# A softplus table by another name, and column sums added along the rows of y

## The chip, the core and the metric

The kernel runs on one core of a Trainium2 chip. The core has engines that run side by side, each with a queue of its own[...]: TensorE (PE: matmuls, results in PSUM), VectorE (DVE: elementwise work and scans), ScalarE (ACT: activation functions), GpSimd (POOL), and SyncE (SP), which here only issues DMA transfers. Engines wait for each other through semaphores. The metric is the device time of the whole program in microseconds; less is better.

## The reference

Four layers run one after the other on a tensor of 4 images, 192 channels, 56 x 56 pixels. The change lies in the fourth, a selective scan over the image in four directions (L is the number of pixels, D the channels, N = 4 states):

```
xs = stack([x_hw, x_wh, x_hw[..., ::-1], x_wh[..., ::-1]])       # by rows, by columns, both reversed
dts, Bv, Cv = split(einsum('kcd,bkdl->bkcl', x_proj_w, xs))
dt = softplus(einsum('kdr,bkrl->bkdl', dt_proj_w, dts) + dt_proj_b)
h  = exp(dt * A) * h + dt * Bv * u          # step by step along L
y_k = sum over the states of h * Cv         # plus Ds * xs
y  = y_0 + flip(y_2) + columns to rows(y_1) + columns to rows(flip(y_3))
out = x + out_proj(layer_norm(y) * silu(z))
```

So each of the four directions gives one value for each channel and pixel, and y is their sum. The values of the two column directions come in the order of columns, while y is kept in the order of rows.

## The kernel before

The 192 channels are kept as two halves of 96 partitions (`h` = 0, 1). An image of 3136 pixels is cut into seven chunks of 448 (`SCH`): for the row directions (`o == 0`) a chunk is 8 rows of 56, for the column directions (`o == 1`) it is 8 columns of 56. `steps` lists image, direction and chunk: for each image the rows forward, the columns forward, the columns backward, the rows backward, seven steps each.

The work of the layer is written as Python generators. `begin` makes the inputs of a row chunk (layer norm, projection, a 3 x 3 convolution as nine matmuls of L1851, Silu); `begin_columns` makes the products of the column directions with the matmuls of L1893 and the copy of L1896; `load` fetches a step's inputs; `sizes` makes dt for two steps at a time, with a matmul (L1985) and a Softplus (L1997); `decay` spreads dt over the states by DMA (L2023) and takes exp (L2031); `scan` does the rest; `final` normalizes y (matmuls of L1768, VectorE at L1770 and L1789, ScalarE at L1912, matmuls of L1929) and writes the output.

In `scan`, for one half of one step: VectorE multiplies dt and u into `du` (L2046 for rows, L2049 for columns, where u is read 56 floats apart); PE spreads `du` over the states (L2056); VectorE multiplies by B in place in PSUM (L2062) and scans (L2078); GpSimd multiplies by C (L2085); PE sums the four states into a PSUM bank `py` (L2101); and VectorE adds that to `y`: at L2106 for the first direction, at L2111 for the rows backward, at L2114 for both column directions.

The order of all instructions comes from `Order`, a planner that runs while the program is built. Each piece of work names an engine and a cost; `Order.run` picks the piece that could start first and writes it into the queues. ScalarE's functions come from table sets, of which one is loaded at a time. A piece may name the set that it needs. If it differs from the last name, the planner counts `SWITCH` = 1.3 us and issues a load of that set (the line of the helper shows as L315 in the profile):

```
            if table and table != self.table:
                self.table = table
                self.nc.scalar.preload_act_table_set(table)
```

Where an activation finds that the set before it doesn't hold its function, a load is put in front of it when the program is compiled, and stands under the activation's own line. The names are constants (L349 and L350); layer 4 uses `EXP_LN`, `SILU` and `SOFTPLUS`.

Of the kernel before, what the change touches and what calls it, by code (L numbers as in the profile page):

```python
# [19 lines left out]
B, C, H, W = 4, 192, 56, 56  # L20
HW = H * W
HALF = 96
# [214 lines left out]
def rows2(ap, w=W):  # L237
    return ap.rearrange("p (y x) -> p y x", x=w)


class Order:
# [20 lines left out]
    def take(self, kind="bank"):  # L262
        slot = min((s for s in self.kinds[kind] if s[0] is not None), key=lambda s: s[0])
        slot[0] = None
        return slot[1]

    def done(self, tile):

        (slot,) = (s for slots in self.kinds.values() for s in slots if s[1] is tile)
        slot[0] = self.end + self.LATENCY  # L270
# [53 lines left out]
def on_pe(n, *takes, ready=None):  # L324

    return "PE", 0.0019 * n, takes, None, ready


def on_dve(*n, takes=(), ready=None):
    return "DVE", sum(0.08 + 0.00105 * i for i in n), takes, None, ready  # L330


def on_scan(n, ready):
    return "DVE", 0.1 + 0.0023 * n, ("st",), None, ready
# [6 lines left out]
def on_pool(*n, each=0.0011):  # L341
    return "POOL", sum(0.2 + each * i for i in n), (), None, None
# [4 lines left out]


EXP_LN, GELU = "natural_log_exp_and_others", "gelu_and_others"  # L349
SILU, SOFTPLUS = "silu_and_others", "softplus_and_others"  # L350


def layers01(tc, x_in, packs, aps, dst):
# [1322 lines left out]
def layer3(tc, src, packs, aps, dst):  # L1676
# [7 lines left out]
    nc = tc.nc  # L1684
    with ExitStack() as ctx:
# [74 lines left out]
        def gone(*what):  # L1760
            return what in passed
# [244 lines left out]
        def use(t, h):  # L2006

            users[t, h] = users.get((t, h), 0) + 1
            if users[t, h] == 2:
                done(sized[t][0][h])  # L2010
# [23 lines left out]
        def scan(t, h):  # L2034

            b, o, s, c = steps[t]
            u = us[b % 2]
            head = c == (NSC - 1 if s else 0)
            last = c == (0 if s else NSC - 1)
            px = slice(c * SCH, (c + 1) * SCH)  # L2040
            yield lambda: t in sized and (2 * t + h == 0 or gone("multiplied", 2 * t + h - 1))
            dts, b_, c_ = sized[t]
            yield on_dve(SCH, takes=("du",))
            du = take("du")
            if o == 0:
                nc.vector.tensor_mul(du, dts[h], u[:HALF, h, px])  # L2046
            else:
                uv = u[:HALF, h].rearrange("p (y x) -> p x y", x=W)[:, 8 * c : 8 * c + 8]
                nc.vector.tensor_mul(rows2(du, H), rows2(dts[h], H), uv)  # L2049
            use(t, h)  # L2050

            yield on_pe(500, *["bank"] * 3)
            tiles = [take() for _ in range(3)]
            for j in range(3):
                r = slice(32 * j, 32 * j + 32)
                nc.tensor.matmul(tiles[j][:, :SCH], w["c96.rep"][r], du[r], start=True, stop=True)  # L2056
            done(du)
            passed.add(("multiplied", 2 * t + h))
            ends = []
            for j in range(3):  # L2060
                yield on_dve(SCH, ready=order.end if j else None)
                nc.vector.tensor_mul(tiles[j][:, :SCH], tiles[j][:, :SCH], b_)  # L2062
                ends.append(order.end + order.LATENCY)
            if h == 1:
                done(b_)
            das, sts = [], []
            for j in range(3):
                g = 3 * h + j
                yield lambda: (t, h, j) in decays and (head or (t - 1, g) in states)
                da, at = decays.pop((t, h, j))  # L2070
                yield on_scan(SCH, ready=max(at, ends[j]))
                sts.append(take("st"))
                r = slice(None, None, -1 if s else 1)
                first = 0.0
                if not head:
                    before = states.pop((t - 1, g))
                    first = before[:, 0:1] if s else before[:, SCH - 1 : SCH]
                nc.vector.tensor_tensor_scan(  # L2078
                    sts[j][:, r], da[:, r], tiles[j][:, :SCH][:, r], first, ALU.mult, ALU.add
                )  # L2080
                done(tiles[j])
                if not head:
                    done(before)
                yield on_pool(SCH, each=0.0021)
                nc.gpsimd.tensor_mul(da, sts[j], c_)  # L2085
                das.append(da)
                if last:
                    done(sts[j])
                else:
                    states[t, g] = sts[j]  # L2090
            if h == 1:
                done(c_)
                del sized[t]

            yield lambda: b == 0 or gone("read", b - 1, c if (o, s) == (0, 0) else 0)
            yield lambda: (o, s) == (0, 0) or len(started) == 2 * NSC * (b + 1)
            yield lambda: s == 0 or o == 1 or added[b] >= 6 * NSC + 2 * (NSC - 1 - c) + h
            yield on_pe(600, "bank")
            py = take()
            for j in range(3):  # L2100
                nc.tensor.matmul(py[32 * j : 32 * j + 32, :SCH], w["c128.sum"], das[j], start=True, stop=True)  # L2101
                done(das[j])
            yield on_dve(SCH)
            sums = py[:HALF, :SCH]
            if (o, s) == (0, 0):
                nc.vector.scalar_tensor_tensor(  # L2106
                    y[:HALF, h, px], u[:HALF, h, px], d_sum[:, h : h + 1], sums, ALU.mult, ALU.add
                )
                started.add((t, h))
            elif o == 0:  # L2110
                nc.vector.tensor_add(y[:HALF, h, px], y[:HALF, h, px], sums)  # L2111
            else:
                yv = y[:HALF, h].rearrange("p (y x) -> p x y", x=W)[:, 8 * c : 8 * c + 8]
                nc.vector.tensor_add(yv, yv, rows2(sums, H))  # L2114
            done(py)
            added[b] += 1
            if o == 0 and s == 1 and h == 1:
                passed.add(("summed", b, c))
            if added[b] == 8 * NSC:
                passed.add(("scanned", b))  # L2120
# [9 lines left out]
        for t in range(len(steps)):  # L2130
            order.add(2 * t - 5, load(t))
            if t % 2 == 0:
                order.add(2 * t - 3, sizes((t, t + 1)))
            for h in range(2):
                order.add(2 * t + h - 1, decay(t, h))
                order.add(2 * t + h, scan(t, h))
# [35 lines left out]
```

## Time and profile before

| | |
|---|---|
| median of 3 runs | 7017.2 us (7013.4 to 7018.1) |
| the profiled execution | 7014.4 us |
| its span, first to last instruction | 7012.6 us |
| last layer, about | 5050 to 7013 us |
| busy in the span: PE / DVE / ACT / POOL | 5931.5 / 5950.0 / 2699.1 / 1408.0 us |
| table loads under L315 | 358 of 1.283 us |
| table loads under L1997 | 71 of 1.283 us |
| add of L2114 (columns) | 112 of 0.982 us |
| add of L2111 (rows) | 56 of 0.607 us |

The profile is of one execution. A row of a group gives line, engine, operation, the tiles written and read, their shape and number; then, behind the bar, the time that the group kept its engine busy and the mean of one in ns; then how long the engine sat idle before such instructions and what ended that. A row of a stretch gives its limits, its length, and the busy time of each engine in it with the number of instructions, then the granted TensorE clock, the busy share of the DMA engines and what they moved. In the chain of waits a row is start, length and what ran; "issue" is time in which the engine waited for nothing that the profile shows. A row of a line's own view gives shortest, median and longest in ns.

### The profile page before, as it was taken

How to read it: one execution, taken by the hardware profiler on the slowest of the kernel's cores; microseconds unless marked ns; L12 is line 12 of the kernel's file. 1: busy time of each engine (PE TensorE's matmuls, PEld its weight loads, DVE VectorE, ACT ScalarE, POOL GpSimd, SP SyncE). 2: the span in 40 equal slices, each digit the busy share in tenths (PEclk: the TensorE clock that was granted, in tenths of full speed). 3: DMA queues.
4: the chain of work that ended last, by engine and by line, in shares of the span. 5: the costliest groups of instructions: out<-in, count | busy, mean ns of one | idle time of the engine just before them, and what ended most of it. 6: DMA issues, size and time to landing. Idle time of an engine off the chain costs nothing.

```text
span 7012.6 us, 107574 instructions
## 1 busy us (share of the span) xinstructions
PE 5931.5 (85%) x43810; PEld 2703.5 (39%) x43810; DVE 5950.0 (85%) x7379; ACT 2699.1 (38%) x4134; POOL 1408.0 (20%) x1409
## 2 busy tenths in 40 slices
PE   4999989999999994877888888875888999888856
PEld 2444444444544441344444454442322322222212
DVE  2799999999999999548999989997269779698697
ACT  1111111222212221144455555553356666566544
POOL 0000000000000000032222122210235445355354
PEclk9999989999999997989999999997999999999977
DMA  3222112221222112210000000000246555465454
GB/s 93 56 52 68 31 32 60 52 68 29 63 51 66 35 43 70 64 32 16 17 20 15 19 16 19 18 13 7 60 116 152 135 130 147 115 151 147 118 131 112
DMA packets 252043, 462.68 MB, mean 66 GB/s; under 512 B 30388, under 2 KB 237964, under 8 KB 240412
## 3 DMA queue, kind: packets, MB, share of 16 engines
q1 hardware_dynamic: 251548, 455.80, 25.6%
q8 instruction: 345, 5.65, 0.3%
q14 instruction: 150, 1.23, 0.1%
HBM read 238.58 MB, written 62.96 MB: 43 GB/s over the span
## 4 chain that ended last, share of the span: by engine, by line
DVE 47%; PE 36%; issue 7%; ACT 5%; POOL 2%; DMA 2%; SPq 0%; DVEq 0%; POOLq 0%; ACTq 0%
DVE pr L789 9%; DVE oa L794 6%; PE a_bank L634 5%; DVE bg L1343 5%; PE c_bank L1851 4%; DVE ob L794 4%; DVE st L2078 3%; DVE bxn L1343 3%; PE c_bank L2056 2%; PE a_bank L884 2%; PE a_bank L869 2%; PE c_bank L1893 2%; PE c_bank L2101 2%; DVE c_bank L2062 2%; PE c_bank L1929 2%
## 5 line engine op out<-in xcount | busy, mean ns | idle before, releaser
L789 DVE TENSOR_TENSOR pr<-vdx,attn 112x1792 f32<-112x1792 f32 (+4 forms) x720 | 1185.9, 1649 | 19.0
L634 PE MATMUL a_bank<-qk_in,w_a 64*49 64x392 f32 x9408 | 1158.6, 496 | 0.0
L2085 POOL TENSOR_TENSOR da<-st,bc 128x448 f32<-128x448 f32 x672 | 845.4, 1267 | 884.9 <-DVE st L2078 793.7
L794 DVE TENSOR_TENSOR oa<-oa,pr 112x1792 f32<-112x1792 f32 (+1 forms) x423 | 765.1, 1809 | 0.0
L634 PE MATMUL a_bank<-qk_in,wd 64*49 64x392 f32 x4032 | 694.6, 496 | 0.0
L2078 DVE TENSOR_TENSOR_SCAN st<-da,st,c_bank 128x448 f32<-128x448 f32 x576 | 644.7, 1133 | 20.9 <-issue 12.7
L634 PEld LDWEIGHTS a_bank<-qk_in,w_a 64*49 64x49 f32 x9408 | 431.7, 120 | 395.9 <-issue 391.2
masks.py:197 POOL MEMSET b_ident<- 128x128 f32 x1 | 0.2, 206 | 2861.2 <-DVE sc L1042 2861.2
L2031 ACT ACTIVATE da<-da,a_neg 128x448 f32<-128x448 f32 x672 | 407.4, 658 | 155.8 <-DMA da<-dt 144.6
L315 ACT ACT_TABLE_LOAD x358 | 459.3, 1283 | 6.2
L2062 DVE TENSOR_TENSOR c_bank<-c_bank,bc 128x448 f32<-128x448 f32 x672 | 385.3, 619 | 75.3 <-PE c_bank L2056 74.5
L2056 PE MATMUL c_bank<-du,w_c 32*128 32x448 f32 x1344 | 291.3, 663 | 173.9 <-DVE du L2049 96.4
L1343 DVE SCALAR_TENSOR_TENSOR bg<-bzpad,w_b,bg 128x448 f32<-128x448 f32 (+2 forms) x672 | 421.8, 682 | 0.0
L1851 PE MATMUL c_bank<-pad,diag 128*96 128x448 f32 (+2 forms) x1008 | 413.0, 549 | 2.4 <-ACT pad L1832 2.4
L2101 PE MATMUL c_bank<-da,w_c 128*32 128x448 f32 x1344 | 343.8, 612 | 73.9 <-POOL da L2085 60.3
L794 DVE TENSOR_TENSOR ob<-ob,pr 112x1792 f32<-112x1792 f32 (+3 forms) x282 | 393.3, 1395 | 0.0
L869 PE MATMUL a_bank<-xc,w_a 128*128 128x448 f32 x672 | 300.8, 577 | 70.2 <-DVE xc L854 70.2
L878 ACT ACTIVATE hm<-a_bank,w_a 128x448 f32<-128x448 f32 x168 | 106.4, 634 | 644.9 <-PE a_bank L869 619.1
L634 PEld LDWEIGHTS a_bank<-qk_in,wd 64*49 64x49 f32 x4032 | 249.1, 120 | 256.4 <-issue 254.5
L1432 PE MATMUL bank<-bxn,w_b 128*128 128x448 f32 (+2 forms) x672 | 295.0, 567 | 16.7 <-DVE bxn L1215 16.3
L884 PE MATMUL a_bank<-hm,w_a 128*96 128x448 f32 x672 | 289.3, 562 | 21.1 <-ACT hm L878 21.1
L586 ACT ACTIVATE qk_in<-a_bank,qk_bias,qk_scale 64x224 f32<-64x224 f32 (+5 forms) x288 | 146.3, 526 | 412.2 <-PE a_bank L571 409.9
(306 smaller groups left out, 10091.6 us busy)
## 6 DMA issues: line engine op xcount, KB each, us to landing
da<-dt SPq DMA_DIRECT2D x672, 224.0 KB
vdx<-vmem SPq DMA_DIRECT2D x168, 476.0 KB
bc<-prod SPq DMA_DIRECT2D x224, 224.0 KB
row<-x SPq DMA_DIRECT2D x56, 336.0 KB
x<-x SPq DMA_DIRECT2D x4, 2352.0 KB
vmem<-vt SPq DMA_DIRECT2D x56, 168.0 KB
xc<-x SPq DMA_DIRECT2D x56, 168.0 KB
mid<-xc SPq DMA_DIRECT2D x56, 168.0 KB
```

The costliest lines, as they stand in the source:

```text
L315: self.nc.scalar.preload_act_table_set(table)
L634: nc.tensor.matmul(py[a][outs[g], : 7 * W].rearrange("p (y x) -> p y x", x=W), wt[halves[a], dx], q[halves[a], r, i0 + m : i0 + m + 7, dx ...
L789: nc.vector.tensor_mul(pr, vv, wt)
L794: nc.vector.tensor_add(og, og, before)
L869: nc.tensor.matmul(ph[:, :CH], w["a128.c1T"][:, k, 128 * m : 128 * m + 128], xt[:, k], start=(k == 0), stop=(k == 1),)
L1343: nc.vector.scalar_tensor_tensor(dst, x, wt[:, t : t + 1], dst, ALU.mult, ALU.add)
L1851: nc.tensor.matmul(rows2(pc[:HALF, : n * W]), diag[:, h, t], pad[:, h, at + t // 3 : at + t // 3 + n, t % 3 : t % 3 + W], start=(t == 0), ...
L2056: nc.tensor.matmul(tiles[j][:, :SCH], w["c96.rep"][r], du[r], start=True, stop=True)
L2062: nc.vector.tensor_mul(tiles[j][:, :SCH], tiles[j][:, :SCH], b_)
L2078: nc.vector.tensor_tensor_scan(sts[j][:, r], da[:, r], tiles[j][:, :SCH][:, r], first, ALU.mult, ALU.add)
L2085: nc.gpsimd.tensor_mul(da, sts[j], c_)
L2101: nc.tensor.matmul(py[32 * j : 32 * j + 32, :SCH], w["c128.sum"], das[j], start=True, stop=True)
```

## The change

Two edits in the last layer. The constant `SOFTPLUS` names the set "softplus" in place of "softplus_and_others". And the add of L2114 runs through the same elements of `y` in another order: before, along the 56 pixels of a column and then over the 8 columns, with the sums read from PSUM in their own order; after, along 8 neighbours in a row and then over the 56 rows, with the sums read from PSUM 56 floats apart. The number of elements and their values are the same, as are the costs and names that the planner compares.

```
-SILU, SOFTPLUS = "silu_and_others", "softplus_and_others"
+SILU, SOFTPLUS = "silu_and_others", "softplus"
...
             else:
-                yv = y[:HALF, h].rearrange("p (y x) -> p x y", x=W)[:, 8 * c : 8 * c + 8]
-                nc.vector.tensor_add(yv, yv, rows2(sums, H))
+
+                yv = y[:HALF, h].rearrange("p (y x) -> p y x", x=W)[:, :, 8 * c : 8 * c + 8]
+                nc.vector.tensor_add(yv, yv, sums.rearrange("p (x y) -> p y x", y=H))
             done(py)
```

## The prediction

> **What bounds the kernel now.** I began with the page: the program is a row of stages, and both edits act in the last layer alone (about 5050 to 7013 us), so whole-span shares say little. I cut that stretch at the places where the column-direction steps begin and end, and asked for the busy time of each engine in each piece.
>
> ```profile
> core 0: us, PE busy (x) PEld busy (x) DVE busy (x) ACT busy (x) POOL busy (x), PEclk, DMA share, GB/s
> 5050.00:5230.00 180.00, 168.45 (x494) 52.82 (x492) 102.67 (x136) 105.85 (x147) 58.11 (x54) 0.97 0.45 113
> 5230.00:5425.00 195.00, 169.81 (x585) 49.79 (x586) 187.60 (x230) 122.70 (x176) 108.54 (x89) 0.95 0.59 147
> ...
> 6190.00:6390.00 200.00, 172.42 (x598) 50.22 (x593) 192.25 (x237) 127.18 (x183) 111.73 (x93) 0.95 0.60 150
> ...
> 6675.00:6880.00 205.00, 126.02 (x400) 29.50 (x400) 188.36 (x228) 93.78 (x135) 115.71 (x86) 0.74 0.53 132
> ```
>
> The first row is a row-direction piece: PE works 168 of 180 us, and DVE has room. The other three are column pieces, and there are four, one for each image: DVE works 187.6 of 195, 188.2 of 196, 192.3 of 200 and 188.4 of 205 us, while PE has 25 us or more free. So the columns are VectorE's and the rows are TensorE's. In the first column piece the longest wait of PE is for VectorE: 16.2 us, before the matmuls of L2056, for `du` of L2049. ScalarE is nowhere full (at most 64%), so table loads cost only where others stand still for them.
>
> Next the groups by line, shapes kept apart, and the single lines of the two edits:
>
> ```profile
> L2062 DVE TENSOR_TENSOR c_bank<-c_bank,bc 128x448 f32<-128x448 f32 x672 | 385.3, 619 | 75.3 <-PE c_bank L2056 74.5
> ...
> L2049 DVE TENSOR_TENSOR du<-dt,u 96x448 f32<-96x448 f32 x112 | 113.6, 1014 | 0.0
> L2114 DVE TENSOR_TENSOR y<-y,c_bank 96x448 f32<-96x448 f32 x112 | 109.9, 982 | 12.9 <-PE c_bank L2101 12.6
> ...
> L2111 DVE TENSOR_TENSOR y<-y,c_bank 96x448 f32<-96x448 f32 x56 | 34.0, 607 | 30.6 <-PE c_bank L2101 30.6
> ```
>
> ```profile
> L1997 ACT ACT_TABLE_LOAD  x71: 1283/1283/1283, 5050.2 to 6915.4; - x71
> ```
>
> ```profile
> L1655 DVE TENSOR_TENSOR bacc<-bacc,bank x400: 401/409/420, 3063.3 to 4737.0; 96x256 f32<-96x256 f32 x134
> ```
>
> L2114 is the edited add. L2111 is the same add for the row directions, same sizes and memories, without a stride: 607 against 982 ns. The second fence is a table load under the line of the Softplus itself, 71 times; the third is an add of the layer before, which edit 2 needs. Last the chain of waits, where one of them stands:
>
> ```profile
> 5169.77 1.28 ACT L315
> 5171.05 0.01 issue
> 5171.06 1.28 ACT L1997
> 5172.34 0.01 issue
> 5172.35 0.64 ACT dt L1997
> 5172.99 0.02 issue
> 5173.02 0.63 DVE du L2046
> ```
>
> Two loads run back to back: the one that the planner asks for (L315), and then another under L1997. The first does nothing useful.
>
> **What the edits leave alone.** The planner sees table names only as equal or unequal and charges one SWITCH for a change; the add's cost is `on_dve(SCH)` both times. So the order of every queue, SP's and POOL's too, stays as it is; no instruction or DMA is moved or added, and no semaphore wait is new. Shorter work in an unchanged order lets later work start earlier, never later, unless it collides: the `da` transfers behind a Softplus (SP, L2023) start up to 1.3 us sooner, with DMA busy 0.45 to 0.6, which has room.
>
> **Edit 1, the table name.** If "softplus" holds the function, the 71 loads under L1997 go: 71 x 1.283 = 91.1 us of ScalarE. The loads back to exp and ln (L315) stay. Identity, as in the activations of L1912 that follow a Softplus, already runs from the softplus table, so no load comes back there. What is it worth? Reading the chain through the last layer, 13 of the 71 lie on it, ten in full and three for 0.15 us with the rest put under "issue", so at most 13 x 1.283 = 16.7 us. In the place shown, `du` and the matmuls of L2056 follow the Softplus within 0.04 us each, so all of the load is won there, and the next late thing is the copy of the products (L1896) ahead of it. Elsewhere it is the matmul that feeds the Softplus: in the last image nine Softplus wait another 2.8 to 5.2 us for L1985 after the load, which is then hidden whole. How close the next cover stands at the 13 the chain does not say. Bounds 0 (nothing is added that could cost) and 16.7; I take 11, two thirds.
>
> The Trainium skill, page "ScalarE: Activation LUTs", section "What ACT_TABLE_LOAD costs", adds a drain of about 1.38 us to each switch, 2.66 in all. Here the Softplus starts 12 ns after the load ends in 53 of 71 cases, so the trace has no such drain. By the page the 13 would be worth 34.6 us, by the trace 16.7; I use the trace.
>
> **Edit 2, the add.** Before, `y` is read and written in SBUF 56 floats apart and the sums stream from PSUM in order. After, `y` goes in runs of 8 floats, and the sums are read from PSUM 56 floats apart. Runs of 8 in SBUF cost nothing: L1655 reads and writes such runs with its other operand in PSUM, and needs 409 ns for 256 elements, against 607 for 448. The two differ by 198 ns for 192 elements, 1.03 ns each, as in a plain stream. The strided PSUM read is the unknown, as no VectorE row of this trace has one.
> Low end: it is free, 607 ns (no less, since 448 elements at 1.03 ns leave no room below), a gain of 112 x 0.375 = 42 us of VectorE. High end: it costs what the SBUF stride does, or more. L2049 strides one read only and takes as long as L2114 (medians 981 and 982), so one strided read is enough to lose the gain.
> Against the change stands the skill: "Advanced Engine Details and Errata", section "PSUM Cachelines", gives PSUM lines of 8 bytes, and wants every two elements in a row for best throughput. Every element would now be on a line of its own: 982 ns stays, or more. For the change stands L2062: it reads and writes PSUM in place, two accesses for each element, at 619 ns, no slower than L2111 with one. So PSUM has some access rate to spare, where the SBUF rows show none that covers a stride. I take 607 ns as the likelier, at six in ten, no more.
>
> Of the 42 us, how much shows? Low: the chain has pieces of L2114 in 50 places, 50 x 0.375 = 18.8 us. High: in the column pieces VectorE is busy 756 of 796 us, 95%, and 0.95 x 42 = 40. Between 5280 and 5330 us five of eight adds are on the chain, which would make 26. Once VectorE is 10 us shorter an image, PE (170 of 195) and the POOL products (L2085) set more of the steps. I take 24.
>
> **Sum.** 24 + 11 = 35 us. The profiled execution took 7014.4 us (span 7012.6 and 1.8 around it), 2.8 below the median of 7017.2; a 35 us cut makes it 6979 and the median 6982. A measurement of this kernel tells about 0.2%, 14 us, from no change.
>
> **The rivals.**
> - *PSUM stride costs as in SBUF* (982 stays): only the loads count, 0 to 17, middle 11: 7006, which is mostly no change. For it the skill's rule; against it L2062.
> - *PSUM stride costs two steps*: lines half as wide, so 607 + 2 x 375 = 1357 ns, 375 more than now. It falls in the column pieces, where VectorE is the bound; 70% of 112 adds on the way to the end (the cover shrinks as VectorE grows) make 78 x 0.375 = +29, less 11 for the loads: +18, 7035. It turns slower from about 11 / 78 = 0.14 us above 982, so from 1.12 us an add. For it: the skill's narrower lines. Against it: the one known stride costs just one step.
> - *The name doesn't do what it says*: "softplus" too is followed by a load under L1997. Then only the add counts, about 24: 6993. The profile cannot exclude it; it shows only that the present name doesn't serve.
>
> **How the numbers follow.** Full-rate PSUM read 0.60, its own range 6968 (all 16.7 and some 32 of the add) to 7001 (18.8 with no load); PSUM as SBUF 0.26; two steps 0.10; useless name 0.04. Faster by over 0.2%: 0.58 + 0.07 of the second case + 0.03 = 0.68. Within 0.2%: 0.02 + 0.18 + 0.01 + 0.01 = 0.22, one term for each case in this order. Slower: 0.09 of the two-step case and 0.01 of the second. The range 6968 to 7015 takes in the first two cases and leaves out the two-step one, with a few tails.
>
> **What would show it right or wrong.** L1997 should have no ACT_TABLE_LOAD left, and L315 still 358. L2114's successor (L2115, as a line is added) should stand near 607 ns; 980 or 1350 decides for a rival. VectorE's busy time should fall by 42 us and the four column pieces shorten by 5 to 8 us each, with more waits of L2062 for the matmuls of L2056. ScalarE should lose 91 us of busy time for about 11 of the span. The prediction fails if the add is at 607 and the column pieces keep their length, or if PE's waits grow by as much as VectorE saves.

## The result, and the profile after

The changed kernel took 6971.6 us (median of 5 runs, 6968.4 to 6974.9) against 7017.2 before: a ratio of 0.9936, with an interval of 0.9921 to 0.9950. That is 45.6 us less. In a second set of runs the same pair gave 0.9949 (0.9935 to 0.9962), 37.5 us. The forecast was 35 us, in a range that holds both.

The page of the profile after, its first lines, and the rows of the two edits (the views of the lines themselves, then the groups of the last layer with their shapes):

```profile
span 6966.6 us, 107498 instructions
## 1 busy us (share of the span) xinstructions
PE 5909.1 (85%) x43810; PEld 2697.8 (39%) x43810; DVE 5902.2 (85%) x7379; ACT 2605.9 (37%) x4063; POOL 1402.8 (20%) x1409
```

```profile
L2115 DVE TENSOR_TENSOR y<-y,c_bank x112: 581/600/619, 5215.9 to 6825.4; 96x448 f32<-96x448 f32 x112
```

```profile
L315 ACT ACT_TABLE_LOAD  x358: 1283/1283/1283, 207.7 to 6871.5; - x179
```

```profile
L2062 DVE TENSOR_TENSOR c_bank<-c_bank,bc 128x448 f32<-128x448 f32 x672 | 384.6, 617 | 89.7 <-PE c_bank L2056 89.3
...
L1997 ACT ACTIVATE dt<-c_bank,w_c 96x448 f32<-96x448 f32 x224 | 128.9, 625 | 132.3 <-PE c_bank L1985 130.6 <-DVE du L2046 0.8
...
L2115 DVE TENSOR_TENSOR y<-y,c_bank 96x448 f32<-96x448 f32 x112 | 67.3, 601 | 16.4 <-PE c_bank L2101 16.3
```

And the row of the Softplus before, with the same shapes, for comparison:

```profile
L1997 ACT ACTIVATE dt<-c_bank,w_c 96x448 f32<-96x448 f32 x224 | 128.9, 626 | 73.6 <-PE c_bank L1985 72.4
```

Both edits do what they say. The add is at 600 ns (before 982) and VectorE lost 47.8 us of busy time, 42.6 of it here. All 71 loads under L1997 are gone, ScalarE is 93 us less busy, and L315 still has its 358. But look at what stands in front of the Softplus now: it waits 130.6 us for its matmuls of L1985, where before it waited 72.4. Of the 91 us of loads, 58 became waiting (80 in the pair of experiments below that differs by the name alone and has the new add: 54.8 to 134.8 us). And L2062 waits 89.3 us for L2056, before 74.5, as forecast.

The stretches of the last layer, cut at the first `du` and the last add of an image's columns (the row stage before them, then the columns of the first, third and last image):

```profile
5046.00:5200.30 154.30, 146.88 (x423) 45.74 (x421) 84.95 (x114) 79.64 (x115) 47.50 (x46) 0.98 0.43 109
5200.30:5400.20 199.90, 176.92 (x629) 53.85 (x628) 189.63 (x244) 123.34 (x184) 116.28 (x96) 0.96 0.60 151
6141.30:6342.30 201.00, 177.96 (x629) 54.06 (x628) 189.76 (x245) 123.44 (x184) 116.32 (x96) 0.95 0.60 150
6614.10:6825.40 211.30, 133.91 (x416) 31.44 (x416) 186.69 (x237) 89.83 (x137) 120.78 (x90) 0.69 0.52 130
```

The columns are still VectorE's (190 of 200 us), but the last image gained little: cut in the same way it took 214.5 us before and 211.3 now, at a granted TensorE clock of 0.69. That is the odd one, and the experiments come back to it.

Of the 46.0 us between the two profiled spans, only 34.0 arise in the last layer. It begins (first instruction of L1722) at 4911.0 us in the profile before and at 4899.0 us in the one after, behind layers that the change does not touch.

### The profile page after: what moved, and what is told of

Its sections match the earlier page's. It is cut to its first block, busy times and chain, and to the rows that moved or that the text cites. A ratio compares the mean times of both kernels' runs of the same rounds, so it can differ in the third digit from the quotient of the medians.

```text
span 6966.6 us, 107498 instructions
## 1 busy us (share of the span) xinstructions
PE 5909.1 (85%) x43810; PEld 2697.8 (39%) x43810; DVE 5902.2 (85%) x7379; ACT 2605.9 (37%) x4063; POOL 1402.8 (20%) x1409
## 4 chain that ended last, share of the span: by engine, by line
DVE 46%; PE 38%; issue 6%; ACT 6%; DMA 2%; POOL 2%; SPq 0%; DVEq 0%; POOLq 0%; ACTq 0%
DVE pr L789 9%; DVE oa L794 6%; PE a_bank L634 6%; DVE bg L1343 5%; PE c_bank L1851 5%; DVE ob L794 4%; DVE st L2078 3%; DVE bxn L1343 3%; PE c_bank L2056 2%; PE a_bank L884 2%; PE c_bank L1893 2%; PE a_bank L869 2%; PE c_bank L2101 2%; PE c_bank L1821 2%; PE c_bank L1929 2%
## 5 line engine op out<-in xcount | busy, mean ns | idle before, releaser
L2062 DVE TENSOR_TENSOR c_bank<-c_bank,bc 128x448 f32<-128x448 f32 x672 | 384.6, 617 | 89.7 <-PE c_bank L2056 89.3
L2056 PE MATMUL c_bank<-du,w_c 32*128 32x448 f32 x1344 | 285.3, 666 | 162.4 <-DVE du L2049 88.5
L1851 PE MATMUL c_bank<-pad,diag 128*96 128x448 f32 (+2 forms) x1008 | 414.8, 551 | 2.4 <-ACT pad L1832 2.4
L655 PE MATMUL a_bank<-qk_sum,w_a 64*49 64x168 f32 (+1 forms) x5376 | 277.2, 337 | 27.8 <-DVE qk_sum L625 25.8
```

Source lines behind the costliest of these rows:

```text
L1851: nc.tensor.matmul(rows2(pc[:HALF, : n * W]), diag[:, h, t], pad[:, h, at + t // 3 : at + t // 3 + n, t % 3 : t % 3 + W], start=(t == 0), ...
```

## The experiments

**One edit at a time, and a control.** The table name alone:

> Only the table name is changed; the add keeps its strided form. The whole change took 45.6 us off the median; between the two profiles 34 us of that arose in the last layer and 12 us before it starts (4911.0 to 4899.0 us), in layers that neither edit touches. Theory (as predicted): the 71 loads are worth 11 us of the last layer, 0 to 16.7; the 12 us ahead of it are chance between executions, so this kernel is 11 us faster and its last layer begins within 5 us of the one before. First rival: a program with one table set less runs its first three layers faster too; then the last layer begins some 10 us sooner here, in the profile and in the median (about 22 us faster in all), and not in the kernel with the add alone. Second rival: the loads are worth the whole 34 us and the add nothing: 34 us faster or more.

The add alone:

> Only the add is changed; the table name and its double loads stay. Theory: 112 adds at about 601 ns in place of 982 save 42.7 us of VectorE, of which about 24 us show: 6993. First rival (the table set also speeds up the first three layers): the same 24 us here, but the last layer begins where it did before. Second rival (the add is worth nothing): no change, 7017. If VectorE is the bound without a break in the column pieces, up to 40 us: 6977.

Both edits again:

> The changed kernel again, on the same chip as the others: 40 to 46 us faster than before, of which 34 us in the last layer. Theory: the gains of the two edits in the last layer add up to this within 4 us, since they bear on different pieces (rows and columns). If they cover each other, the sum of the parts is larger than the whole; if each opens the way for the other, smaller.

And the kernel before as it is:

> The kernel before, unchanged, as a control with a profile of its own: ratio 1.000 within 0.002. Theory: the start of its last layer (4911.0 us in the first profile) differs by several us from one execution to the next, so the 12 us between the two profiles ahead of the last layer are chance, at least in part. Rival: it starts within 2 us of 4911.0, and the 12 us belong to the change.

| kernel | median us | ratio to before (interval) | last layer in its profile |
|---|---|---|---|
| table name alone | 7015.2 | 0.9998 (0.9990 to 1.0006) | 4902.1 to 7010.8 |
| add alone | 6987.4 | 0.9961 (0.9948 to 0.9973) | 4915.0 to 6992.6 |
| both | 6979.4 | 0.9949 (0.9935 to 0.9962) | 4901.6 to 6972.4 |
| control | 7017.3 | 1.0001 (0.9993 to 1.0009) | 4901.7 to 7013.6 |

The add alone brings 29.5 us, near the forecast of 24. The table name alone brings nothing that can be measured; beside the add it brings another 8 us (6987.4 to 6979.4, with intervals that overlap). The parts, 2 and 29.5, make 31 of 37.5. The difference of 6 us lies within the intervals, so that the two edits help each other is not shown.

The control answers the question of the first three layers. The unchanged kernel, too, began its last layer at 4901.7 us, 9.3 us earlier than in its other profile, and still ended 1.0 us later. So the 12 us ahead of the last layer are of the size that two executions of one kernel differ by. The rival that a program with one table set less runs its first layers faster falls: the control, with the old name, is as early there as the table name alone (4902.1) and both edits (4901.6). The same pair of profiles warns that the length of the last layer, 2101.6 and 2111.9 us in two profiles of one kernel, is not to be trusted to 10 us from one profile.

The pieces tell more than the sums, since most repeat to a few tenths of a us where the granted clock is the same. Length in us, and granted TensorE clock:

| piece | before | control | table name alone | add alone | both again | after |
|---|---|---|---|---|---|---|
| columns, image 2 | 207.8 / 0.94 | 207.6 / 0.94 | 208.4 / 0.94 | 202.4 / 0.94 | 200.9 / 0.95 | 200.9 / 0.95 |
| columns, image 4 | 214.5 / 0.74 | 214.5 / 0.75 | 213.5 / 0.72 | 202.7 / 0.87 | 214.2 / 0.62 | 211.3 / 0.69 |
| rows backward, image 2 | 148.8 / 0.94 | 152.5 / 0.91 | 149.8 / 0.92 | 150.8 / 0.93 | 146.7 / 0.95 | 146.6 / 0.95 |
| rows forward, image 2 | 115.2 / 0.97 | 115.1 / 0.97 | 117.0 / 0.93 | 115.2 / 0.97 | 114.0 / 0.97 | 113.9 / 0.97 |

(All from start to start. Columns: first `du` of L2049 to the last add of the columns. Rows backward: from there to the last add of L2111. Rows forward: first add of L2106 to the first `du` of L2049. "Before" and "control" are two profiles of one kernel, "both again" and "after" of the other.) The add takes 5.2 us off the columns of image 2 and 11.8 off those of image 4. The table name is harder to see. Its rows backward are 2.7 us shorter than the control's, but 1.0 longer than those of the other profile of the unchanged kernel, so this gain is not shown; beside the add it takes off 4.1. Alone it lengthens the rows forward by 1.9, where the clock is lower than in the control and a matmul of L1851 takes 577 ns in place of 548. And in the columns of the last image both edits together are 11.5 us slower than the add alone: there a gain elsewhere was given back.

Why? The row of that last piece, the VectorE waits (us in total, times, longest) and the TensorE groups, first of the add alone, then of both:

```profile
6649.60:6852.40 202.80, 113.33 (x416) 26.91 (x416) 185.60 (x238) 99.13 (x143) 120.92 (x90) 0.87 0.54 136
```

```profile
DVE c_bank L2062 <- PE c_bank L2056: 10.6, 16, 1.0
DVE y L2115 <- PE c_bank L2101: 5.8, 14, 0.6
```

```profile
L2101 PE MATMUL c_bank<-da,w_c 128*32 128x448 f32 x180 | 65.9, 725 | 37.5 <-POOL da L2085 26.4 <-DVE st L2078 11.1
L2056 PE MATMUL c_bank<-du,w_c 32*128 32x448 f32 x180 | 37.6, 702 | 52.0 <-DVE du L2049 46.2 <-DVE du L2046 5.7
L1985 PE MATMUL c_bank<-dr,w_c 64*96 64x448 f32 x56 | 12.2, 555 | 0.0
```

```profile
6616.80:6831.10 214.30, 141.39 (x416) 32.42 (x416) 186.88 (x238) 89.90 (x137) 120.73 (x90) 0.62 0.52 129
```

```profile
DVE c_bank L2062 <- PE c_bank L2056: 19.8, 30, 1.0
DVE y L2115 <- PE c_bank L2101: 6.8, 14, 0.9
```

```profile
L2101 PE MATMUL c_bank<-da,w_c 128*32 128x448 f32 x180 | 73.6, 855 | 23.9 <-POOL da L2085 23.6
L2056 PE MATMUL c_bank<-du,w_c 32*128 32x448 f32 x180 | 49.4, 909 | 49.0 <-DVE du L2049 43.3 <-DVE du L2046 5.7
L1985 PE MATMUL c_bank<-dr,w_c 64*96 64x448 f32 x56 | 22.3, 950 | 0.0
```

The number and the order of the matmuls are the same, but one matmul of L2056 takes 909 ns in place of 702, one of L1985 950 in place of 555. The scans and products of VectorE, ScalarE and GpSimd keep their durations within a few ns. VectorE waits 30 times, not 16, for the matmuls of L2056: 9.2 of the 11.5 us stand in that one row, another 1.0 in the next. The clock records of this piece change between 1.0 and 0.5 in steps of 3.4 us: 53 us of it at 0.5 with the add alone, 161 with both.

Read one by one against the clock records, the matmuls tell the cause. In both kernels L2056 takes 584 ns in the mean where the clock is 1.0, and 1024 (add alone) or 1028 ns (both) where it is 0.5. With the add alone 48 of the 180 start at 0.5, with both 132, and this alone makes the means of 702 and 909. Nor is it one execution: over the whole program the granted clock was 0.923 to 0.926 in the five executions of the add alone, and 0.917 to 0.920 in the five of both edits beside them.

What keeps the clock low with both edits was not found. It is not a longer rest of TensorE: in both traces it stands idle in this piece eight times, for about 6.0 us each time. With the add alone the clock goes to 0.5 near the end of each of these pauses, for 6.8 us, and then stays at 1.0 until the next; with both it falls back to 0.5 in between. The changed kernel does not always do it to the same degree: 161 us in one profile, 131 in the other (after).

**Keeping TensorE busy in that piece, first try.** Small matmuls of constants, behind the sums:

```
+            if b == B - 1 and o == 1:
+                for _ in range(8):
+                    nc.tensor.matmul(py[:HALF, SCH:512], ones, diag[:, 0, 0, :64], start=True, stop=True)
```

> The changed kernel, and in the column steps of the last image eight small extra matmuls (96 x 64, into unused columns of the bank) behind the sums of L2101; they add work of TensorE and nothing to the result. New theory, from the granted clock of the pieces: the column piece of the last image took 202.7 us at a clock of 0.87 with the add alone, but 214.2 at 0.62 and 211.3 at 0.69 with both edits, so TensorE, left idle longer, runs it at half speed for more of the time and gives back about 10 us. With the extra matmuls the clock of this piece should rise to 0.85 or more and the piece should take 200 to 204 us: 7 to 12 us faster than with both edits, about 6965. Rival: the piece is bound by VectorE and the clock is only a symptom; then the extra matmuls cost nothing or up to 56 x 1 us of TensorE that has room, and the piece stays at 211 to 215 or grows.

It failed: 7029.3 us, a ratio of 1.0013 (1.0006 to 1.0019), 8 us slower than before in its set of runs, where both edits were 37.5 us faster than before in theirs. The piece took 265.9 us and its clock stayed at 0.69. Each of the 448 small matmuls takes 297 ns and has a weight load of 206 ns (medians), and the add, which reads the bank that they write, waits 54.4 us for them in this piece; with both edits it waited 6.8. So the run tells nothing of the clock's effect on the piece; but more instructions in TensorE's queue did not by themselves raise the clock.

**Second try: wide matmuls,** 448 columns, where TensorE waits for GpSimd:

```
             py = take()
+            if b == B - 1 and o == 1:
+                for _ in range(1):
+                    nc.tensor.matmul(py[:HALF, :SCH], ones, u[:, 0, :SCH], start=True, stop=True)
             for j in range(3):
```

> The changed kernel with one extra matmul (96 x 448) into the bank of the sums, ahead of the sums of L2101 that overwrite it, at each of the 56 half steps of the last image's columns: work of TensorE alone, without effect on the result, placed where TensorE waits for GpSimd. 56 x 0.42 = 24 us of TensorE in a piece where it has about 70 us free. If the half clock is what costs the piece 9 to 11 us (211 to 214 against 202.7 with the add alone), a clock of 0.8 or more here brings 203 to 207 us. If the clock stays at 0.62 to 0.69 the piece stays at 211 or grows by up to 20, and the question stays open; if it rises and the piece doesn't shorten, the clock is not the cause.

And with `range(2)`:

> The same with two extra matmuls at each half step: 47 us of TensorE. The clock should be higher still, 0.9 or more, and the piece 200 to 205 us if the clock is the cause; from some number on the extra work costs more than the clock gives, at the latest when TensorE has no room, and then the piece is longer than with one.

With one, of 722 ns and 35 us in all (24 were expected): 6981.1 us, 0.9940 (0.9928 to 0.9953), the same as both edits within the intervals; the piece 213.9 us at a clock of 0.83. With two: 6988.4, 0.9951 (0.9939 to 0.9964); 224.3 us at 0.86. So the clock can be raised this way, but the piece did not get shorter, and by the expectation the clock would not be the cause of its length. The waits show why that reading is too quick. VectorE's waits in the piece, with one extra matmul:

```profile
DVE y L2118 <- PE c_bank L2104: 16.7, 14, 2.3
DVE c_bank L2062 <- PE c_bank L2056: 10.7, 16, 1.0
```

The wait for L2056 (matmuls at 715 ns again) is back from 19.8 us to 10.7, as the 10.6 of the add alone; but the sums (L2104 here) now stand behind the extra matmul, and the add waits 16.7 us for them in place of 6.8. The 9.1 us won are paid again as 9.9. With two it is the same again: L2056 at 703 ns, the wait for it 9.8 us, the wait for the sums 28.1. So the clock does set what VectorE waits for L2056, by these two runs and the durations above; but a run in which the piece gets shorter by a higher clock alone was not found, and the theory's first step, that TensorE is left idle longer, is not borne out by the pauses.

**The queue of SyncE.** The prediction said that its order stays. That is wrong: the planner fixes four engines, and the DMA issues of SyncE are ordered by the framework. With the table name changed, 55 of its 1889 issues stand in another place, most of them of L2023, L1964 and L1970; with the add alone none does. The order of the other engines is the same in all four kernels. To see whether that ate the gain, SyncE was put under the planner's order as well, with the old name and with the new:

```
-        engines = {mybir.EngineType.PE, mybir.EngineType.Activation, mybir.EngineType.DVE, mybir.EngineType.Pool}
+        engines = {mybir.EngineType.PE, mybir.EngineType.Activation, mybir.EngineType.DVE, mybir.EngineType.Pool, mybir.EngineType.SP}
```

> The kernel before, with SyncE's queue too written in the planner's order. Found since: the planner fixes the order of four engines only; SyncE's queue is ordered by the framework from its own estimate of durations, so the table name alone reorders some of the DMA issues of the last layer, which the prediction had excluded. Here the order is the same for both table names, and this run is the base for the next. Its own time may lie some per cent to either side of 7017.

> The same with the table name changed: all queues are those of the run before it but for the 71 loads. If the reordered DMA issues had eaten the gain of the table edit, it shows here as the predicted 11 us (up to 17) against that run. If the gain is eaten by the matmuls at half speed, or the loads were covered, it is within 5 us of that run, as it was (2 us) without the fixed order.

7031.6 us (1.0013, 1.0007 to 1.0020) and 7025.3 (1.0004, 0.9996 to 1.0012). With the order held, the table name brings 6.3 us, between the 2 of the first pair and the 8 beside the add: neither the 11 forecast nor within the 5 of the rival. The reordering may cost a few us of the gain; the intervals do not separate 2 from 6. So at most a part of what is missing from the 11 went there. The last image's columns are long in both of these kernels (226 and 225 us, at clocks of 0.64 and 0.65), so this pair says nothing of what happens there beside the new add.

**More loads instead of fewer,** on the kernel before:

```
                 self.nc.scalar.preload_act_table_set(table)
+                if table == SOFTPLUS:
+                    self.nc.scalar.preload_act_table_set(EXP_LN)
+                    self.nc.scalar.preload_act_table_set(table)
```

> The kernel before, with two more table loads at each switch to softplus (four in a row in place of two): 2 x 71 x 1.283 = 182 us of ScalarE added. If the loads were off the way to the end, as the table edit alone suggests (2 us of 91), up to 10 us slower. If they were on it and the edit's gain was given back elsewhere, the loads show here by their full on-chain share: 26 x 1.283 = 33 us slower or more. Above 33 us: more of them come onto the chain as they grow.

7132.6 us, 1.0155 (1.0142 to 1.0169): 111 us slower for 182 us of loads, 61% of them. Only the last line of the expectation, more loads coming onto the chain as they grow, holds. The columns of image 2 grew from 207.6 to 223.8 us. So a load is nearly free when one of two is taken away and dear when two are added. That fits a slack of about one load at these places, as the wait of the Softplus for L1985 says: it is 72.4 us in all with the old double loads, 1.0 for each of the 71 places, and 36.3 with four. The 111 us are not the loads' alone, though: SyncE's issues are reordered here too, 70 of the 1889.

**The PSUM stride by itself.** The sums read in order, added to the wrong pixels:

```
-                nc.vector.tensor_add(yv, yv, sums.rearrange("p (x y) -> p y x", y=H))
+                nc.vector.tensor_add(yv, yv, sums.rearrange("p (y x) -> p y x", y=H))
```

> The changed kernel with the sums read from PSUM in their own order while y still goes in runs of 8 floats along its rows; this adds the sums to the wrong pixels and is for the duration of the add alone. If PSUM's stride is free, the 112 adds take the same 600 ns as with the stride (within 10 ns), and the whole time is that of both edits. If the stride has a price that is covered at 600, they drop towards 560 or less.

```profile
L2115 DVE TENSOR_TENSOR y<-y,c_bank x112: 581/604/619, 5229.0 to 6841.3; 96x448 f32<-96x448 f32 x112
```

604 ns in order, 600 with 224 bytes between the elements. The strided read from PSUM is free in this add. (Its one execution took 6984.4 us as a whole, near the 6979.4 of both edits in another set.)

**A version without the softplus table.** Softplus as Exp and Ln of 1 + x, on top of both edits:

```
-                    yield on_act(SCH, takes=("dt",), table=SOFTPLUS)
+                    yield on_act(SCH, SCH, takes=("dt",), table=EXP_LN)
                     dts.append(take("dt"))
-                    nc.scalar.activation(
-                        dts[h], tiles[h][:HALF, :SCH], AF.Softplus, bias=w["c96.dt_b"][:, h, k : k + 1]
-                    )
+                    pt = tiles[h][:HALF, :SCH]
+                    nc.scalar.activation(pt, pt, AF.Exp, bias=w["c96.dt_b"][:, h, k : k + 1])
+                    nc.scalar.activation(dts[h], pt, AF.Ln, bias=one)
```

> The changed kernel with the Softplus as Exp and then Ln of 1 + x, both of the set that the exponentials of L2031 use: all softplus loads and the loads back go (about 2 x 71 of 1.283 us = 182 us of ScalarE), and 224 activations of about 0.63 us are added (141 us). The planner sees other costs and may order the queues anew. If the time of ScalarE spent in loads still bounds the rows, 5 to 15 us faster than both edits. If ScalarE has not been the bound since the first 71 loads went, as the table edit alone suggests with 2 us, then within 5 us of both edits, either way; a new order alone may move it by 10 us.

6893.8 us, 0.9815 (0.9801 to 0.9828): 128 us below before and far below both edits, while 5 to 15 or nothing was expected. The loads in the last layer fall from 186 to 57:

```profile
L2001 ACT ACTIVATE dt<-c_bank,c_one 96x448 f32<-96x448 f32 x224 | 141.2, 631 | 7.3
L2000 ACT ACTIVATE c_bank<-c_bank,w_c 96x448 f32<-96x448 f32 x224 | 132.5, 591 | 208.5 <-PE c_bank L1987 208.2
L315 ACT ACT_TABLE_LOAD x57 | 73.1, 1283 | 1.0
```

ScalarE's busy time in the last layer falls by only 47 us against the changed kernel (1091 to 1044), while the layer gets 87 us shorter (2067.6 to 1980.3). The planner no longer sees the switches to softplus and writes all queues in another order. Rows backward of image 2 went from 146.6 to 115.9 us, with some of their work moved into the piece behind them, and the granted clock there from 0.95 to 0.99. How much is owed to the order, to the loads and to the clock was not separated. It is the fastest version of this study.

## Why the prediction was right, and where its steps were off

- *The add at 607 ns, by a strided PSUM read at full rate*: right, 600, and shown by the read in order at 604. The Trainium skill's rule ("Advanced Engine Details and Errata", section "PSUM Cachelines": two elements in a row for best throughput) is not borne out for this add; the row that was weighed against it, L2062, pointed the right way, though at 619 ns it is 12 ns slower than L2111 and not "no slower". Both rivals built on that rule fall.
- *What of the 42 us shows, 24*: 29.5 measured, inside the bounds of 18.8 and 40. The columns shortened by 5.2 us in image 2 with the add alone, as said (5 to 8), and by 11.8 in the last image, where the clock was higher too.
- *The loads, 11 us of 16.7*: the weakest step. Alone 2, with SyncE's order held 6, beside the add 8. The on-chain count was a bound, as stated, but "two thirds" had nothing behind it. The cover that the prediction named, the matmuls of L1985, took more than a third: 58 of the 91 us became waiting for it, 80 beside the add. Beside the add, part of the rest was given back at TensorE's half clock.
- *ScalarE nowhere full, at most 64%*: misread. That holds for the rows shown; in the rows-backward pieces of the same view it was busy 70% (73.0 of 105 us). Those are the pieces that the name shortens beside the add.
- *The order of every queue, SP's too, stays*: wrong for SyncE with the table name. Small in its effect, but the premise was not checked in the code: the engines that the planner orders are listed at its call, and SyncE is not among them.
- *Shorter work lets later work start earlier, never later*: wrong as a rule. The durations of the matmuls themselves grew in the last columns, at a lower clock, and the piece took 11.5 us longer than with the add alone.
- *The sum of 35*: 37.5 in the second set, 45.6 in the first. The second is made of an add that was sized 5 us too small and a load term sized 3 too large; that the two misses cancel in part is luck. Why the first set shows 8 us more is open; the two intervals (0.9921 to 0.9950, 0.9935 to 0.9962) overlap. Of the 5.8 us between the profiles of the two sets, 2.6 arise ahead of the last layer and 2.9 in the columns of the last image, whose clock was 0.69 in the one and 0.62 in the other. The lower end of the gain was summed wrongly: 18.8 us with no load makes 6998, not 7001; nothing hangs on it.

## What to carry to other kernels

An add or multiply with one operand in SBUF and one in PSUM can put its stride on the PSUM side: measure it, here it cost nothing where the SBUF stride cost 375 ns of 982. Before counting a removed instruction, look at what its engine waits for right behind it; time that turns into a longer wait for the same event is no gain. And check which queues a hand-made order really covers before arguing that an order stays.

## What was not expected of the hardware

The granted TensorE clock, 0.5 or 1.0 in steps of 3.4 us, can lengthen a piece that is VectorE's: L2056 took 702 ns in one kernel and 909 in another with the same TensorE instructions in the same order and the same eight pauses of 6.0 us, because 132 in place of 48 of its 180 matmuls fell into records of 0.5. The 96 x 64 matmuls, each behind its weight load, left the clock at 0.69; one 96 x 448 matmul at each half step raised it to 0.83, two to 0.86. And two executions of one kernel reached the last layer 9.3 us apart and yet ended within 1.0 us of each other.
